# A two-layer GRU and a mixture of experts on one core: another opening, another spread of side work over the steps, and other ends

## The chip, the cores and the metric

The kernel runs on one core of one Trainium2 chip. The metric is device microseconds of one execution; the runs' median is given with its lowest and highest. The profile is of one more execution, with its own time. Engines: PE multiplies matrices, DVE (VectorE) and ACT (ScalarE) work on elements, POOL (GpSimd) issues the indirect DMAs and some small work, SP (SyncE) issues most other DMAs.

## The reference, cut to what matters

Two batches of 1024 tokens, 256 wide. A layer `x = x + L0(x, cond)`, then `x = x + L1(x, cond)`:

```python
# L0
mixed = tanh(x @ W_in.T + b_in + cond)
# a GRU layer: h starts at 0, one step per token
r = sigmoid(xr + hr); z = sigmoid(xz + hz)
n = tanh(xn + r * hn)
h = (1 - z) * n + z * h
# two such layers, one on the other; then
gate = sigmoid(cond @ W_gate.T + b_gate)
out = ((gate + 1) * h2) @ W_out.T + b_out
# L1: 8 experts, 2 of them for each token
shared = (silu(x @ w1) * (x @ w3)) @ w2
s = sigmoid(concat(x, cond) @ router_W)      # top 2 of s + router_bias
routed = sum over the chosen: s_e / sum(s) * (gelu(x @ W1e[e]) @ W2e[e])
out = (shared + routed) / 3
```

## The kernel before

**The recurrence in chunks.** Each sequence is cut into J = 16 chunks of S = 62 tokens, and all 2 x 16 = 32 chunks take a step at once. A chunk's begin is not known, so each layer first takes warm-up steps: `AHEAD = (62, 44)`. Whether all chunk ends fit the begins is counted; if not, a second path (not run here) computes it step by step. The 2048 tokens lie in 64 groups of 32, a group being what one step takes. The first 32 tokens are two extra groups, 0 and 1 (`EXTRA = 2`).

**A tick** is one turn of the loop at L666: a step of layer 0, and from tick 20 on a step of layer 1 that follows it by `LAG = 2`. Ticks 0 to 123 run layer 0, 20 to 125 layer 1. In a step (`finish_scanned`, L320), PE adds the state's product with `whh` (L289) to sums that hold the input's part already; ACT makes the two gates (L330); a DVE scan makes r * hn + xn (L333); ACT's tanh makes n (L344); DVE makes (z - 1) * h (L346); a second scan makes the new row (L349); and DVE transposes it (L362) for the next product. Hooks between these (`before_n`, `after_n`, `between`) take other work, in the order in which the engine's queue gets it. The sign of z's part and of n's weights is turned once, in the weights themselves (`negate`, L193).

**Side work in the ticks.** The step's input comes from `inputs` (four parts per group: bias of the state's part, then r, z, n). Two kinds of pieces make it. A mixing piece (`mix`, L229) makes half of `mixed` for 256 tokens: four products on PE (L238), two tanh on ACT (L250). An input piece (`input_piece`, L418) makes one group: 16 products on PE (L261) and a DVE addition of the biases (L428). `work_of` (L550) gives each tick before layer 1 runs room for three, where a mixing piece counts two, and each later tick one piece, in the order of `pieces_in_turn`; mixing so reaches into the ticks with both layers. `prepare` (L502) has ACT copy a group's inputs into the sums' bank for the next tick (L506); `feed` (L511) adds layer 1's input products (L261 as well).

**Places.** `place(tick, where, what)` hangs other work at a spot of a tick: `product` (on PE, behind layer 0's state product), `n0`, `scan0`, `scan1` (in the hooks of the first or second layer), `end`. Before the change `Front.prepare` (L822: the output gate, the gated output weights, the condition's part of the router) stands at ticks 12 to 16, and the output products of finished groups of 8 (`plan`, L604) follow from tick 71 on. Everything in the loop is issued in the written order (`manual_schedule`, L665).

**Start.** SP's queue loads `w_in`, the first 256 tokens of x, `wih0`, its bias, `whh0`, 256 more tokens, the second bias, `wih1`, `whh1`, the rest of x (1.5 MB in three), then what is used later. Two mixing pieces, DVE's negation in `wih0` and two input pieces stand ahead of tick 0.

**The end of the loop and after.** w1's products for the first part of the shared expert's hidden layer stand at tick 125, its w3 products in `all_of` (L970) for the last group of 8: output products, x added, then the turn to token order, then the router's products. `moe` routes (L1060 to L1195), computes the shared hidden parts, gathers tokens of each expert's block with POOL's indirect DMAs (L1251), multiplies (L1222), writes rows to DRAM (L1268), and gathers them back (L1312), 32 gathers. From the ninth on a one-element POOL copy (L1311) stands ahead of a gather and reads something made just before, which holds the gather behind it. In the last loop (L1340) a product of `w2` per 128 tokens, two gathered rows added (L1326), the sum (L1352), and SP's output DMA (L1353).

Of the kernel before, what the change touches and what calls it, by code (L numbers as in the profile page):

```python
# [17 lines left out]
P = 128  # L18
B = 2
# [22 lines left out]
EXTRA = FIRST // J  # L42

# [40 lines left out]
def gru_moe(ctx, tc, xT, vec, bias, w_in, wih0, whh0, wih1, whh1, w_out, w_gate, router, w1, w3, w2, w1e, w2e, out):  # L84
# [62 lines left out]
    class Steps:  # L147


        def __init__(self, stack, tag, on_pe, rest_of_x):  # L150
# [13 lines left out]
            wih0_sb = weights(wih0, KD, 3 * D, "wih0_sb", gru_only)  # L164
            load_bias(0)
            whh0_sb = weights(whh0, KD, 3 * D, "whh0_sb", gru_only)
# [25 lines left out]

        def negate(self, engine, weights_sb, i):  # L193

            part = weights_sb.rearrange("p k (q g u) -> p (k q) g u", q=Q, g=3)[:, :, i, :]
            engine.tensor_scalar(part, part, -1.0, None, ALU.mult)  # L196
# [32 lines left out]
        def mix(self, n0):  # L229

            mixed = self.mixed_pool.tile([P, KD, MB], FP, name="mixed")
# [22 lines left out]
            return mixed, [piece(m) for m in range(KD)]  # L254
# [65 lines left out]
        def finish_scanned(self, layer, to, tick, before_n, after_n, between, keep=None):  # L320
# [6 lines left out]
            sums = by_sum(ps)  # L327

# [15 lines left out]
            nc.scalar.activation(n[:, :, 0], s[:, 1 : 2 * U : 2], AF.Tanh, scale=-1.0)  # L344
# [13 lines left out]
            if keep is not None:  # L358
                kept = self.edge.tile([P, U], FP, name=f"kept{layer}")
                nc.vector.tensor_scalar(kept, row, keep, None, ALU.mult)  # L360
                row = kept
# [26 lines left out]


    with ExitStack() as stack:  # L390
        g = Steps(stack, "", on_pe=False, rest_of_x=lambda: load_x(MB, TB - MB))
# [6 lines left out]
        for n0 in range(TB, N, TB):  # L398
            load_x(n0, TB)
# [18 lines left out]
        def input_piece(i):  # L418

            ps = g.bank("ps_in")[:, 0 : 3 * U].rearrange("p (c u) -> p c u", c=3)  # L420

            def products():
                at = i * R % MB
                mixed = mixes[i * R // MB]
                return g.times_input(0, ps, lambda k: mixed[:, k, at : at + R], True)

            def rest():
                nc.vector.tensor_tensor(inputs[:, i, 1:4, :], ps, g.sum_bias[0][:, 1:4, :], ALU.add)  # L428
                made.append(i)

            return products, rest, lambda: None
# [28 lines left out]
        nc.vector.tensor_scalar(not_first, not_first, 1.0, None, ALU.min)  # L460
# [72 lines left out]
        mixes, mixed_pieces = {}, []  # L533

        def mix_pieces():
            for i, n0 in enumerate(range(0, N, MB)):
                mixes[i], pieces = g.mix(n0)
                mixed_pieces.extend(pieces)
                yield from pieces

        def input_pieces():
            for i in (*range(EXTRA, MB // R), *range(EXTRA), *range(MB // R, GROUPS)):
                yield input_piece(i)
# [6 lines left out]
        def work_of(tick):  # L550


            if runs(1, tick):
                return take(in_turn, 1)
            room, pieces = 3 - 2 * ((tick, "product") in places), []
            while room > 0:
                new = take(in_turn, 1)
                if not new:
                    break
                pieces += new  # L560
                room -= 2 if new[0] in mixed_pieces else 1
            return pieces
# [6 lines left out]
        def pieces_in_turn():  # L569

            for _ in range(MB // R, GROUPS, MB // R):
                for which in (mixing, making, mixing, *[making] * (MB // R - 1)):
                    yield from take(which, 1)
            yield from making

# [3 lines left out]
        g.negate(nc.vector, g.wih[0], 1)  # L579
        for piece in take(making, 1):  # L580
            for part in piece:
                part()
        g.negate(nc.vector, g.whh[0], 2)
        prepare(0, 0)
        for piece in take(making, 1):
            for part in piece:
                part()
        in_turn = pieces_in_turn()
# [34 lines left out]
        begun = []  # L623

        def begin_hidden():
            pa, last = front.hidden_sums(g.bank, 0, 0, "w1")
            begun.append(pa)
            return last

        place(AHEAD[0] + S + LAG - 1, "product", begin_hidden)  # L630
        for block in range(1, N // MB):
            place(block - 1, "end", lambda block=block: spread(block))
        place(N // MB - 1, "end", lambda: g.sum_of_biases(1, less_z=True))
        for i, (product, end) in enumerate(front.prepare(g.bank)):
            if product:
                place(12 + i, "product", product)
            place(12 + i, "end", end)
# [27 lines left out]
        with tc.manual_schedule():  # L665
            for tick in range(AHEAD[0] + S + LAG):  # L666
# [10 lines left out]
                for layer in now:  # L677
# [3 lines left out]
                    if layer == 0:  # L681
                        last = placed(tick, "product")
                        last = do(work, 0) or last
                        if not busy:
# [6 lines left out]
                            lambda: placed(tick, "n0"),  # L691
                            lambda: copied.append(prepare(0, tick + 1)),
# [5 lines left out]
                    else:  # L698
                        last = feed(tick + 1, range(KD) if busy or 0 not in now else [1])
                        if 0 not in now:  # L700
                            placed(tick, "product")
# [24 lines left out]

            for where in ("n0", "scan0", "end"):
                placed(AHEAD[0] + S + LAG, where)
            sig, silu = (
                g.mixed_pool.tile([P, KD, MB], FP, name="mixed").rearrange("p k n -> p (k n)") for _ in range(2)  # L730
            )
            nc.scalar.activation(sig, begun[0], AF.Sigmoid)
            nc.vector.tensor_tensor(silu, begun[0], sig, ALU.mult)

            def rest_of_hidden():
                pb, _ = front.hidden_sums(g.bank, 0, 0, "w3")
                nc.vector.tensor_tensor(front.hid(0, slice(0, TB)), silu, pb, ALU.mult)

            front.all_of(g.bank, GROUPS // GS - 1, rest_of_hidden)
# [12 lines left out]
    with tc.If(n_fit < P):  # L752
        with ExitStack() as stack:
# [4 lines left out]
            for n0 in range(0, N, MB):  # L758
                mixed, pieces = g.mix(n0)
                for piece in pieces:  # L760
                    for part in piece:
                        part()
# [41 lines left out]
class Front:  # L804
# [17 lines left out]
    def prepare(self, bank):  # L822
# [16 lines left out]
        def gates():  # L839
            for m in range(KD):  # L840
                nc.scalar.activation(
                    self.gate[:, m, :], ps["gate"][:, m, :], AF.Sigmoid, bias=vec_sb[:, B_GATE + m : B_GATE + m + 1]
                )
            nc.vector.tensor_scalar(self.gate, self.gate, 1.0, None, ALU.add)

        def weights(b):
            for k in range(KD):
                nc.vector.tensor_scalar(
                    self.gated_out[:, b, k, :], later["w_out"][:, k, :], self.gate[:, k, b : b + 1], None, ALU.mult
                )  # L850

        def spread():
            for k in range(KD):
                for b in range(B):
                    i = COND + k * B + b
                    nc.vector.tensor_copy(
                        self.cond_b[:, k, :, b, :], vec_sb[:, i : i + 1].unsqueeze(2).to_broadcast([P, P // R, J])
                    )

        def context_sums():  # L860
# [11 lines left out]

        return (
            (gate_sums, gates),
            (None, lambda: weights(0)),
            (None, lambda: weights(1)),
            (None, spread),
            (context_sums, lambda: nc.vector.tensor_copy(self.context, ps["context"])),
# [91 lines left out]
    def all_of(self, bank, group, between=lambda: None):  # L970
# [4 lines left out]
        between()  # L975
# [452 lines left out]
```

## Time and profile before

| | us |
|---|---|
| median of 3 runs | 540.21 (539.62 to 541.03) |
| profiled execution | 539.22 |
| its span, first to last instruction | 537.4 |
| granted TensorE clock, mean | 0.994 |

Busy times of the stages, in us, from the trace's windows:

| stage | from : to | PE | DVE | ACT | POOL |
|---|---|---|---|---|---|
| to the end of tick 0's second scan | 0 : 13.42 | 8.38 | 4.34 | 3.91 | 2.35 |
| layer 0 alone | 13.42 : 67.74 | 53.53 | 37.17 | 21.67 | 4.17 |
| both layers, mixing | 67.74 : 118.22 | 50.01 | 42.21 | 29.55 | 0.43 |
| both layers | 118.22 : 358.09 | 231.24 | 209.93 | 146.25 | 0.61 |
| last two steps, last group | 358.09 : 370.29 | 9.80 | 8.54 | 3.45 | 0.00 |
| routing, shared hidden | 370.29 : 400.02 | 29.33 | 26.31 | 6.09 | 7.66 |
| experts | 400.02 : 478.49 | 77.79 | 27.21 | 27.79 | 28.37 |
| shared hidden, gathers back | 478.49 : 501.19 | 22.55 | 11.32 | 5.61 | 15.09 |
| last products, outputs | 501.19 : 530.63 | 27.79 | 18.34 | 0.10 | 20.73 |
| close | 530.63 : 537.38 | 0.00 | 0.00 | 0.00 | 0.00 |

The profile puts instructions down to a line of the kernel and a tile: `PE ps_step L289` is the product of a step's state. In the order of time, a row's first number is its start, the second how long it (or a run of equal ones, `x16`) lasted, and the brackets tell how long the engine was idle before it and what it waited for. Matmul ends are modelled, so a PE that is busy throughout can still have been waited for or have waited. Idle time of an engine that is off the chain costs nothing.

### The profile page before, as it was taken

Reading aid. Unit: us, or ns where it says so; the run is one execution under the profiler, and the core shown is the slowest. Engines: PE = TensorE matmul, PEld = TensorE weight load, DVE = VectorE, ACT = ScalarE, POOL = GpSimd, SP = SyncE. Lnnn points to the kernel's source line nnn. Section 1 sums busy time; section 2 is a strip of 40 time slices with the busy share of each in tenths; the row PEclk is TensorE's granted clock in tenths of the full one; section 3 lists DMA queues with packets and bytes.
Section 4 is the critical chain, followed back from the end, with each engine's and each line's share of the span. In section 5 each row is a group of like instructions: output and inputs, shape, how many; then the busy total and the mean of one; then the engine's idle time right before and its main releaser. Section 6 shows DMA issues by size and latency. Waiting matters only on the chain.

```text
span 537.4 us, 18538 instructions
## 1 busy us (share of the span) xinstructions
PE 510.4 (95%) x7492; PEld 339.5 (63%) x7492; DVE 385.4 (72%) x1292; ACT 244.4 (45%) x832; POOL 79.4 (15%) x136
## 2 busy tenths in 40 slices
PE   6999999999999999999999999989999999999993
PEld 3666666666654445665666656655448888864783
DVE  3776678989988888888889888887973333324852
ACT  2334356566666556566565665642123333341000
POOL 1200000000000000000000000002054444117881
PEclk9999999999999999999999999999999999999997
DMA  8990000000000000000000000002023433213453
GB/s 276 368 291 3 2 3 2 4 2 4 13 3 2 13 2 4 2 22 3 22 23 2 23 8 17 23 1 80 1 59 118 124 123 119 98 50 105 118 163 94
DMA packets 23087, 32.13 MB, mean 60 GB/s; under 512 B 3040, under 2 KB 18528, under 8 KB 22976
## 3 DMA queue, kind: packets, MB, share of 16 engines
q1 hardware_dynamic: 19632, 22.04, 12.2%
q0 software_dynamic: 3216, 8.79, 5.9%
q8 instruction: 63, 1.03, 0.8%
q14 instruction: 32, 0.26, 0.2%
q10 hardware_dynamic: 144, 0.01, 0.0%
HBM read 21.26 MB, written 9.57 MB: 57 GB/s over the span
## 4 chain that ended last, share of the span: by engine, by line
DVE 43%; PE 32%; ACT 10%; POOL 5%; issue 5%; DMA 3%; SPq 0%; POOLq 0%; DVEq 0%; ACTq 0%
DVE row L349 15%; DVE ps_step L333 14%; DVE h L362 9%; ACT n L344 9%; PE ps_h L1222 6%; PE ps_y L1222 6%; PE ps_step L289 5%; PE ps_in L261 5%; POOL inputs L1312 4%; PE ps_w L947 3%; PE ps_mix L238 3%; DMA x_sb<-in_xT 2%; PE ps_hT L1214 1%; PE ps_xT L1214 1%; DMA inputs<-back,slots 1%
## 5 line engine op out<-in xcount | busy, mean ns | idle before, releaser
L289 PE MATMUL ps_step<-whh_sb,h 128*32 128x192 f32 x3616 | 193.0, 331 | 6.7 <-DVE h L362 6.0
L289 PEld LDWEIGHTS ps_step<-whh_sb,h 128*32 128x32 f32 x3616 | 95.0, 109 | 72.6 <-DVE h L362 52.6
L349 DVE TENSOR_TENSOR_SCAN row<-gates,n 128x128 f32<-128x128 f32 x230 | 97.7, 425 | 31.7 <-ACT n L344 30.9
L261 PE MATMUL ps_step<-wih_sb,h 128*32 128x192 f32 x1696 | 103.2, 328 | 4.7 <-ACT ps_step L506 1.7
L333 DVE TENSOR_TENSOR_SCAN ps_step<-gates,ps_step 128x128 f32<-128x128 f32 x230 | 96.7, 421 | 14.6 <-ACT gates L330 14.4
L344 ACT ACTIVATE n<-ps_step 128x64 f32<-128x64 f32 x230 | 53.6, 233 | 112.9 <-DVE ps_step L333 112.9
L330 ACT ACTIVATE gates<-ps_step 128x128 f32<-128x128 f32 x230 | 66.6, 290 | 34.1 <-PE ps_step L289 27.5
L261 PEld LDWEIGHTS ps_step<-wih_sb,h 128*32 128x32 f32 x1696 | 57.5, 109 | 30.9 <-ACT ps_step L506 18.1
L362 DVE STREAM_TRANSPOSE h<-row 128x64 f32<-128x64 f32 x228 | 56.0, 246 | 8.0
L947 PE MATMUL ps_w<-x_sb,w_sb 128*128 128x512 f32 x128 | 57.0, 596 | 0.1
L261 PE MATMUL ps_in<-wih_sb,mixed 128*32 128x192 f32 x1024 | 51.7, 327 | 2.0 <-DVE wih_sb L196 2.0
L1216 DVE COPY hT<-ps_hT 128x256 f32<-128x256 f32 x35 | 14.9, 425 | 48.8 <-PE ps_hT L1214 48.8
L506 ACT COPY ps_step<-inputs 128x256 f32<-128x256 f32 x124 | 48.1, 388 | 2.9 <-DVE inputs L428 2.9
L346 DVE SCALAR_TENSOR_TENSOR n<-gates,row 128x64 f32<-128x64 f32 x224 | 46.8, 209 | 0.0
L261 PEld LDWEIGHTS ps_in<-wih_sb,mixed 128*32 128x32 f32 x1024 | 33.6, 110 | 12.9 <-issue 4.4
L1251 POOL DMA_INDIRECT inputs<-given,pick x35 | 33.3, 953 | 55.0 <-PE ps_xT L1214 31.6
L506 ACT COPY ps_step<-bt 128x256 f32<-128x256 f32 x106 | 39.9, 377 | 3.3
L947 PEld LDWEIGHTS ps_w<-x_sb,w_sb 128*128 128x128 f32 x128 | 23.7, 190 | 27.1 <-issue 25.6
L1222 PE MATMUL ps_h<-w1e_sb,xT 128*128 x140 | 36.1, 380 | 0.7 <-DVE xT L1216 0.7
L1222 PE MATMUL ps_y<-w2e_sb,hT 128*128 x140 | 35.9, 379 | 0.0
L1312 POOL DMA_INDIRECT inputs<-back,slots x32 | 31.5, 984 | 29.2 <-DMA back<-y 20.5
L1222 PEld LDWEIGHTS ps_y<-w2e_sb,hT 128*128 128x128 f32 x140 | 26.5, 190 | 4.6 <-DVE hT L1216 1.0
(175 smaller groups left out, 425.2 us busy)
## 6 DMA issues: line engine op xcount, KB each, us to landing
back<-y SPq DMA_DIRECT2D x35, 128.0 KB, 1.7
w1e_sb<-in_w1e SPq DMA_DIRECT2D x1, 2048.0 KB, 14.9
w2e_sb<-in_w2e SPq DMA_DIRECT2D x1, 2048.0 KB, 18.8
given<-inputs SPq DMA_DIRECT2D x8, 256.0 KB, 2.1
out_dram<-inputs SPq DMA_DIRECT2D x16, 128.0 KB, 2.1
wih_sb<-in_wih SPq DMA_DIRECT2D x2, 768.0 KB, 8.7
whh_sb<-in_whh SPq DMA_DIRECT2D x2, 768.0 KB, 10.1
x_sb<-in_xT SPq DMA_DIRECT2D x3, 512.0 KB, 11.2
```

Of the source, the lines that this page charges most:

```text
L261: last = nc.tensor.matmul(out=out[cols(q), :, :], lhsT=given(k), rhs=self.wih[layer][:, k, q * 3 * U : (q + 1) * 3 * U].rearrange("p (g u) ...
L289: nc.tensor.matmul(out=by_sum(self.sums[layer])[cols(q), 0:3, :], lhsT=self.states[layer][:, k, :], rhs=self.whh[layer][:, k, q * 3 * U : ...
L330: nc.scalar.activation(gates[:, :, :, 1], sums[:, 1:3, :], AF.Sigmoid)
L333: nc.vector.tensor_tensor_scan(s, gates[:, 0, :, :].rearrange("p u i -> p (u i)"), ps[:, 0 : 6 * U : 3], 0.0, ALU.mult, ALU.add,)
L344: nc.scalar.activation(n[:, :, 0], s[:, 1 : 2 * U : 2], AF.Tanh, scale=-1.0)
L346: nc.vector.scalar_tensor_tensor(n[:, :, 1], gates[:, 1, :, 1], 1.0, h, ALU.subtract, ALU.mult)
L349: nc.vector.tensor_tensor_scan(row.rearrange("p u i -> p (u i)"), gates[:, 1, :, :].rearrange("p u i -> p (u i)"), n.rearrange("p u i -> p ...
L362: nc.vector.transpose(to, row)
L506: return nc.scalar.copy(by_sum(banks[layer][tick % 2])[:, 0:4, :], g.sum_bias[1] if layer else inputs[:, group_of(0, tick), :, :],)
L947: last = self.tc.nc.tensor.matmul(out=ps, lhsT=self.later[name][:, k, m * P : (m + 1) * P], rhs=self.x1[:, k, blk * TB : (blk + 1) * TB], ...
L1222: nc.tensor.matmul(out=ps, lhsT=of[:, k, :], rhs=weights_sb[:, bass.ds(e * KD + k, 1), :], start=(k == 0), stop=(k == KD - 1),)
L1312: nc.gpsimd.indirect_dma_start(out=yb, out_offset=None, in_=back[:, :], in_offset=bass.IndirectOffsetOnAxis(ap=slots[:, i % 2, i // 2 : i ...
```

## The change

- `wih0` is loaded in two halves with the bias between them; the three loads of the rest of x move ahead of the second bias, `wih1` and `whh1`.
- Ahead of tick 0 nothing is negated any more. The first two input pieces are multiplied with the plain weights; `less_z` subtracts where the negated weight would have been used, and the first group's sums go from PSUM into tick 0's bank at once. Tick 0's end makes the group's stored inputs and negates `wih0` on DVE; ACT negates `whh0` behind tick 0's tanh.
- `mixed` is written into `hs1`, layer 1's state tensor, instead of a pool of two tiles. `work_of` gives ticks 1 to 14 one mixing and one input piece, 15 to 18 three input pieces, 19 two, later ticks one until they are all made.
- The reset of the first chunk's rows is made ahead of a step, on the state and as the tanh's scale, instead of behind it.
- `Front.prepare` moves from ticks 12 to 16 to ticks 54 to 62, cut into smaller parts, in the hooks rather than at the tick's end.
- w1's first hidden products move to tick 123 and the first half of w3's to tick 124, in a new place `behind` (behind layer 1's products); the silu follows at tick 124's end. In `all_of` the router's products come ahead of the turns.
- The one-element copy stands only ahead of every second gather (11 instead of 23). The outputs are issued from ACT's queue instead of SP's.

```diff
-            wih0_sb = weights(wih0, KD, 3 * D, "wih0_sb", gru_only)
+            wih0_sb = gru_only.tile([P, KD, 3 * D], FP, name="wih0_sb")
+            wih0_v = wih0.rearrange("(k p) m -> p k m", p=P)
+            nc.sync.dma_start(out=wih0_sb[:, 0, :], in_=wih0_v[:, 0, :])
             load_bias(0)
+            nc.sync.dma_start(out=wih0_sb[:, 1, :], in_=wih0_v[:, 1, :])
...
+            if keep is not None:
+                kept = self.edge.tile([P, U], FP, name=f"kept{layer}")
+                nc.vector.tensor_scalar(kept, h, keep, -1.0, ALU.mult, ALU.mult)
+                h = kept
...
-            nc.scalar.activation(n[:, :, 0], s[:, 1 : 2 * U : 2], AF.Tanh, scale=-1.0)
+            nc.scalar.activation(n[:, :, 0], s[:, 1 : 2 * U : 2], AF.Tanh, scale=-1.0 if keep is None else keep)
...
-            if keep is not None:
-                kept = self.edge.tile([P, U], FP, name=f"kept{layer}")
-                nc.vector.tensor_scalar(kept, row, keep, None, ALU.mult)
-                row = kept
...
+        def less_z(ps, to):
+
+            biases = g.sum_bias[0][:, 1:4, :]
+            nc.vector.tensor_tensor(to[:, 0:3:2, :], ps[:, 0:3:2, :], biases[:, 0:3:2, :], ALU.add)
+            nc.vector.scalar_tensor_tensor(to[:, 1, :], ps[:, 1, :], -1.0, biases[:, 1, :], ALU.mult, ALU.add)
...
-                return g.times_input(0, ps, lambda k: mixed[:, k, at : at + R], True)
+                return g.times_input(0, ps, lambda k: hs1[:, k, cols(i)], True)
...
+                if EXTRA <= i < EXTRA + PLAIN:
+                    less_z(ps, inputs[:, i, 1:4, :])
...
-                mixes[i], pieces = g.mix(n0)
...
+                yield from g.mix(n0, hs1[:, :, n0 : n0 + MB])
...
-                return take(in_turn, 1)
-            room, pieces = 3 - 2 * ((tick, "product") in places), []
...
+                return take(making, 1)
+            mixed = take(mixing, 1) if tick else []
+            return mixed + take(making, 1 if mixed or not tick else 2 if runs(1, tick + 1) else 3)
...
-        g.negate(nc.vector, g.wih[0], 1)
...
-        g.negate(nc.vector, g.whh[0], 2)
...
+        first_sums = by_sum(banks[0][0])
+        nc.scalar.copy(first_sums[:, 0, :], g.sum_bias[0][:, 0, :])
+        first_ps = by_part(g.bank("ps_in"))
+        (products, _, _), (next_products, next_rest, _) = input_piece(EXTRA, first_ps), input_piece(EXTRA + 1)
+        products()
+        next_products()
+        less_z(first_ps, first_sums[:, 1:4, :])
+        next_rest()
...
+        place(last_tick - 2, "behind", lambda: begin_hidden("w1", range(KD)))
+        place(last_tick - 1, "behind", lambda: begin_hidden("w3", [0]))
+        place(last_tick - 1, "end", silu)
...
+        place(0, "end", lambda: less_z(first_ps, inputs[:, EXTRA, 1:4, :]))
+        place(0, "end", lambda: g.negate(nc.vector, g.wih[0], 1))
...
+                place(AHEAD[0] - 8 + i, where, what)
+        def negate_first():
+
+            part = g.of_gate(g.whh[0], 2)
+            nc.scalar.mul(part, part, -1.0)
...
+                            lambda: placed(tick, "n0") if tick else copied.append(prepare(0, 1)),
+                            lambda: copied.append(prepare(0, tick + 1)) if tick else negate_first(),
...
+            {"product": gate_sums, "scan1": lambda: spread(0)},
+            {"n0": gates, "scan1": lambda: spread(1)},
+            {"scan0": add_one},
+            *({"scan0": lambda b=b, k=k: weights(b, k)} for b in range(B) for k in range(KD)),
+            {"product": context_sums},
+            {"scan0": keep_context},
...
         between()
+        self.route(bank, group)
+        self.keep_logits(group)
+        behind()
...
-        self.route(bank, group)
-        self.keep_logits(group)
...
-        if behind is not None:
+        if behind is not None and i % 2 == 0:
             nc.gpsimd.tensor_copy(yb[0:1, 0:1], behind[0:1, 0:1])
...
-            nc.sync.dma_start(out=out[j * P : (j + 1) * P, :], in_=base[:, j, :])
+            nc.scalar.dma_start(out=out[j * P : (j + 1) * P, :], in_=base[:, j, :])
```

## The prediction

> **What bounds the kernel now.** I read the page first, then busy times by stage, then the order of time, stage by stage.
>
> ```profile
> PE 510.4 (95%) x7492; PEld 339.5 (63%) x7492; DVE 385.4 (72%) x1292; ACT 244.4 (45%) x832; POOL 79.4 (15%) x136
> ...
> DVE row L349 15%; DVE ps_step L333 14%; DVE h L362 9%; ACT n L344 9%; PE ps_h L1222 6%; PE ps_y L1222 6%; PE ps_step L289 5%; PE ps_in L261 5%; POOL inputs L1312 4%; PE ps_w L947 3%; PE ps_mix L238 3%; DMA x_sb<-in_xT 2%; PE ps_hT L1214 1%; PE ps_xT L1214 1%; DMA inputs<-back,slots 1%
> ```
>
> PE is busy 95%, yet the chain that ends last runs through DVE's scans and transposition and ACT's tanh: a step waits for the step before it. The transposition L362 closes a step, so the distance between two layer-0 rows of L362 is one tick. In the order of time I took all of them: 2.79 to 2.81 us while layer 0 runs alone (ticks 1 to 19), 2.74 with both layers (most of ticks 21 to 61), 2.72 to 2.79 later. The longer ones are what there is to win: tick 1 (3.35), 5 (3.12), 13 and 14 (2.95, 2.96), 20 (3.25), 24, 26, 34, 36 (3.44 to 3.47), 29 (3.03), 32 (2.94), 62 and 64. One of them, in the order of time:
>
> ```profile
> 79.24 0.24 DVE L362 STREAM_TRANSPOSE h<-row 128x64 f32<-128x64 f32 x1
> ...
> 82.71 0.24 DVE L362 STREAM_TRANSPOSE h<-row 128x64 f32<-128x64 f32 x1
> ...
> 83.79 1.13 PE L238 MATMUL ps_mix<-x_sb,w_in_sb 128*128 128x256 f32 x4
> ...
> 84.85 0.86 PE L289 MATMUL ps_step<-whh_sb,h 128*32 128x192 f32 x16
> ...
> 85.44 0.24 DVE L362 STREAM_TRANSPOSE h<-row 128x64 f32<-128x64 f32 x1
> ```
>
> The layer-0 rows are 79.24, 82.71 and 85.44: tick 24 took 3.47, tick 25 2.73. A mixing product at 83.79 holds PE while a layer-1 state, transposed from 84.03 to 84.27, waits for its product until 84.85; so tick 26 will be long too. Start and end, same view:
>
> ```profile
> 9.23 0.43 DVE L196 TENSOR_SCALAR wih_sb<-wih_sb 128x512 f32<-128x512 f32 x1 [5.87 <-DMA wih_sb<-in_wih]
> ...
> 11.84 0.29 ACT L330 ACTIVATE gates<-ps_step 128x128 f32<-128x128 f32 x1
> ...
> 12.54 1.10 PE L238 MATMUL ps_mix<-x_sb,w_in_sb 128*128 128x256 f32 x4 [1.28 <-DMA x_sb<-in_xT]
> ...
> 13.42 0.25 DVE L362 STREAM_TRANSPOSE h<-row 128x64 f32<-128x64 f32 x1
> ...
> 14.25 0.83 PE L289 MATMUL ps_step<-whh_sb,h 128*32 128x192 f32 x16
> ...
> 525.70 0.98 POOL L1312 DMA_INDIRECT inputs<-back,slots x1 [0.27 <-POOL inputs L1311]
> ...
> 527.96 1.03 PE L1344 MATMUL ps_s<-w_sb,inputs 128*128 128x256 f32 x4
> ...
> 529.48 0.48 DVE L1326 SCALAR_TENSOR_TENSOR inputs<-inputs,share 128x256 f32<-128x256 f32 x1 [1.38 <-DMA inputs<-back,slots]
> 529.88 0.75 DVE L1352 SCALAR_TENSOR_TENSOR inputs<-ps_s,inputs 128x256 f32<-128x256 f32 x2
> ```
>
> The first step waits for weights, then for their negation; the end waits for POOL's last gather, not for PE, done at 528.99. POOL then waits for that gather (landed 529.35), and its closing drain runs 531.04 to 536.59, the last thing before the span ends.
>
> **The parts and their costs** (plus is time won).
>
> 1. *Start, +1.3.* Whole weights landed at 9.21, bias at 9.74. The second half now stands behind the bias with the same bytes ahead, so 9.75. PE has done the first half by then; eight products for the second take 0.35 and 0.2 to land (half of a 16-instruction piece, 0.66 apart): 10.35. The negation (0.43) is off this path, two sums in its place: 0.28 (L187's row) and 0.21, overlapping, 0.4. Gates at 10.85, not 11.84. Behind them DVE holds the next piece's two sums (0.4), so the scan starts about 11.45; ACT's copy for tick 1 (0.38) now stands ahead of the tanh, still inside the scan. Transposition about 12.65, against 13.42: 0.77. whh0 (landed 11.71) is negated on ACT behind the tanh, 128x512, about 0.6 by its 0.38 for 256 columns: 12.7, inside the transposition. Tick 0 then has no mixing product that waits for x until 12.42; that held tick 1's step from about 13.72 to 14.25: another 0.53. DVE's added work behind tick 0 (two pairs of sums, 0.4 each, and wih0's negation) ends about 14.05, before tick 1's scan at 14.25. Bounds 0.5 (halves bring nothing) and 1.8 (they land at 9.21). SP has one issue more (0.47), but landings run to 20.97 against issues to 10.1, so bytes set them. The three x loads (1.5 MB) pass bias1, wih1 and whh1: at 768 KB in 1.98 us (14.90 to 16.88) these land 4 us later, POOL's negations follow near 21, needed at tick 20 (67 us). That gap hides them.
> 2. *Preparation out of ticks 12 to 16, +0.3* (2.95 + 2.96 less 2 x 2.79), bounds 0 and 0.33.
> 3. *Two pieces instead of three in tick 19, +0.5.* PE was 0.65 over there; tick 20 goes from 3.25 to 2.77. Bounds 0 and 0.5.
> 4. *Mixing in ticks 1 to 14, +2.9.* Four ticks fall to 2.74: 3.47 + 3.47 + 3.44 + 3.47 - 4 x 2.74. What comes in their place, one input piece per tick up to 52, is free: ticks 38 to 44 carried one at 2.74. A single-layer tick with mixing and one piece has 0.82 + 1.06 + 0.92 = 2.8 of PE, and lasted 2.79 (ticks 4, 9, 10). Bounds 2.3 and 2.9.
> 5. *The kept rows, +0.1.* They cost 0.29 and 0.20 behind the scan (ticks 29, 32). Ahead of the first scan DVE has no gap either (L362 to L333 0.17 to 0.23), so 0.1 to 0.2 comes back, and tanh with a scale per partition gets 0.08 longer (mixed, with a bias per partition, 366 ns; gates of the same size 290). Bounds -0.1 and 0.5.
> 6. *Preparation in ticks 54 to 62, -0.5.* Its DVE parts fit between L346 and L349, as the input sums (0.34) do; two gate activations (0.42) fit in ACT's 0.49 wait. PE's eight gate products (0.98) stand between a four-product row of 0.71 that costs about 0.04 a tick and mixing's 1.13 that costs 0.73; nearest to mixing. Bounds 0 and -0.73.
> 7. *Last ticks, +0.6.* w1's products (1.82) start near 358.1 in a 1.54 us PE gap, so tick 124's step moves from 359.75 to about 359.95; w3's first half (0.9) and the turn hold tick 125 by about 0.3. The last products start near 365.6 instead of 365.82, half of w3 (0.9) behind them is gone: 0.6 by the start of the 64 shared products (370.29), where PE is busy 29.33 of 29.73 to 400.02. Silu's 0.60 and 0.69 fill a gap of DVE before 363.79. The routing chain starts 1 us earlier, but its gathers waited for PE already. Bounds -0.2 and 1.9 (all w1 and half w3 hidden, no delay).
> 8. *Gathers and output queue, +2.2.* Of 23 one-element copies 12 go. A gather behind one starts 1.44 after the last, without one 1.25: 12 x 0.19 = 2.3. The last gather starts near 523.4 and lands near 526.9; the last sum is then held by PE's 528.99, so the output leaves at 529.6 instead of 530.75. If the drain goes with the gather, 2.3; if with the output, 1.15. ACT has finished its last activation at 501.3, nothing is queued behind the outputs. I take 2.2; bounds 1.0 and 2.4.
>
> Sum: 1.3 + 0.3 + 0.5 + 2.9 + 0.1 - 0.5 + 0.6 + 2.2 = 7.4. The profiled execution took 539.22 (span 537.4 and 1.8 around it), so 531.8; the runs' median, 540.21, is 0.99 above it, so 532.8. Bounds alone: 10.4 down to 2.8 won, 529.8 to 537.4.
>
> **The rivals.**
>
> A. *The halves pay a fixed time.* The 9 KB vec_sb, issued at 0.80 with nothing ahead, landed at 2.98: 2.2 us are fixed. If the second half pays that behind the first, it lands near 11.95, the gates come 1.2 later than before, and part 1 turns from 1.3 to -0.9: 535.0. Against it: bias landed 0.53 behind wih0 on the same queue.
>
> [...]
>
> B. *The end hangs on PE and the outputs*, the drain with them: part 8 gives 1.0, so 534.0. For it: PE has no pause from 478.49 to 528.99. Against: SP was through its closing waits at 535.40, the drain at 536.59.
>
> C. *Every tick from 1 to 14 pays for its mixing.* Tick 5 had a scan 0.33 late beside a mixing tanh; 14 x 0.33 = 4.6, so 537.4. Against: the other such ticks had no delay.
>
> D. *Slower: layer 1's transposition waits for PE.* Its target hs1 now also holds the mixed inputs that PE reads. If L362 waited for PE's newest product in that tensor, not for the one that read its columns, it would wait for the feed behind it: in the tick at 149.69 that ended 150.17, half a microsecond. Over the 62 first writes (ticks 20 to 81) that is 31 us: 563.8; from 0.12 a tick on the kernel is slower. Against: from tick 71 on, products read hs1 while L362 writes it, at 2.73 to 2.79.
>
> **How the numbers follow.** Forecast 0.62 (532.8; by itself 530.2 to 534.5), A 0.09, B 0.11, C 0.08, D 0.07, gains that cancel 0.03. Within 0.3% (1.6 us) is about what a measurement of this kernel can tell from no change. Faster 0.90, same 0.03, slower 0.07. The range, 530.2 to 536.8, takes in A and B and most of the bounds, and leaves out C, D and the corners.
>
> **What would show it.** Gates of tick 0 near 10.9 and L362 of tick 1 near 15.5 (part 1); ticks 24, 26, 34, 36 at 2.74 (4); tick 55 about 0.5 long (6); the first of the 64 shared products about 11.7 after tick 123's L362, against 12.2 (358.09 to 370.29; 7); 11 copies L1311, the last gather about 41.4 after the first, against 43.67, and the drain earlier by as much (8). The forecast is wrong if wih0's second half lands past 10.5, if single-layer ticks pass 2.9 with a mixing product, if the two-layer tick is not 2.74, or if the drain does not move.

## The result, and the profile after

The changed kernel took 538.00 us (median of 11, 537.09 to 539.23) where the kernel before took 540.21 (median of 11): a ratio of 0.9952, interval 0.9941 to 0.9964. It is faster by 2.2 us, not by the 7.4 forecast, and lies outside the range of 530.2 to 536.8. In the profiled execution the span is 536.8 us against 537.4.

The page after, its engines and its chain. The chain now breaks off at 476.06; what it holds from there to the end is nearly all PE:

```profile
PE 512.1 (95%) x7492; PEld 341.2 (64%) x7492; DVE 385.1 (72%) x1296; ACT 243.6 (45%) x833; POOL 76.9 (14%) x124
...
PE ps_s L1367 6%; PE ps_w L969 4%; DVE inputs L1375 0%
```

Every line of the code moved down; L369 is the old L362, L341 the gates (L330), L355 the tanh (L344), L360 the closing scan (L349), L526 the copy into PSUM (L506), L981 to L983 the shared expert's activation (L959 to L961), L1335 the gather (L1312), L1334 its one-element copy (L1311), L1349 the addition of the gathered rows (L1326), L1367 the last products (L1344), L1375 the last sums (L1352). In the order of time, the start and ticks 24 to 26:

```profile
10.56 0.28 ACT L341 ACTIVATE gates<-ps_step 128x128 f32<-128x128 f32 x1 [1.53 <-DVE ps_step L434]
...
12.06 0.24 DVE L369 STREAM_TRANSPOSE h<-row 128x64 f32<-128x64 f32 x1
...
14.91 0.24 DVE L369 STREAM_TRANSPOSE h<-row 128x64 f32<-128x64 f32 x1
...
79.61 0.24 DVE L369 STREAM_TRANSPOSE h<-row 128x64 f32<-128x64 f32 x1
...
82.35 0.24 DVE L369 STREAM_TRANSPOSE h<-row 128x64 f32<-128x64 f32 x1
...
85.10 0.24 DVE L369 STREAM_TRANSPOSE h<-row 128x64 f32<-128x64 f32 x1
```

Tick 0 closes at 12.06 instead of 13.42, tick 1 at 14.91 instead of 16.76; ticks 25 and 26 take 2.74 and 2.75 (26 took 3.47). Tick 123 closes at 353.80 instead of 358.09 and the first product of the last stage starts at 496.79 instead of 501.19: 4.4 us were won by then, and the forecast had 5.2. The last stage then lost most of it. Busy times of that stage, before and after (the columns are the engines' busy us, the granted clock of PE, the share of the DMA engines and GB/s):

```profile
501.19:528.98 27.79, 27.79 (x129) 24.13 (x127) 17.19 (x40) 0.10 (x1) 20.73 (x34) 1.00 0.54 158
```

```profile
496.79:503.00 6.21, 6.21 (x30) 5.34 (x29) 0.69 (x1) 0.60 (x1) 4.35 (x8) 1.00 0.30 84
503.00:506.66 3.66, 1.75 (x6) 0.91 (x5) 2.45 (x5) 0.00 (x0) 2.91 (x3) 1.00 0.39 110
506.66:513.50 6.84, 5.60 (x14) 4.49 (x15) 4.71 (x12) 0.00 (x0) 2.48 (x4) 0.50 0.29 92
513.50:531.12 17.62, 17.62 (x82) 15.18 (x80) 9.87 (x24) 0.00 (x0) 8.52 (x12) 1.00 0.53 161
```

The same 16 tiles take 34.33 us instead of 27.79. PE stands still three times (0.46, 1.05 and 1.65 us: 3.16) and has a granted clock of 0.50 for 6.84 us, in which it is busy for 5.60. Over the stage it is busy for 31.17 us instead of 27.79: 3.38 more, and with the pauses the 6.54 lost. The trace shows the order in time: the clock falls at 506.66, 0.40 into the longest pause, after 3.66 us in which PE was busy for 1.75, and is back at 1.00 from 513.50 on. In series 3 below the changed kernel paused for 1.7 us in all, 0.4 at the longest, and kept its clock (0.997 in the mean of the execution, 0.991 here); without copies, in the same series, PE was busy for 33.00 of 49.52 us of this stage, at a mean clock of 0.79. What sets the clock was not shown. What stands beside the pauses, in the order of time, DVE and POOL:

```profile
494.96 1.00 DVE L1349 SCALAR_TENSOR_TENSOR inputs<-inputs,share 128x256 f32<-128x256 f32 x2
500.86 0.69 DVE L982 TENSOR_TENSOR silu<-ps_w,sig 128x512 f32<-128x512 f32 x1 [4.90 <-ACT sig L981]
503.70 0.69 DVE L983 TENSOR_TENSOR inputs<-silu,ps_w 128x512 f32<-128x512 f32 x1 [2.15 <-remote]
...
508.65 0.42 DVE L1375 SCALAR_TENSOR_TENSOR inputs<-ps_s,inputs 128x256 f32<-128x256 f32 x1 [2.43 <-remote]
...
509.90 0.42 DVE L1375 SCALAR_TENSOR_TENSOR inputs<-ps_s,inputs 128x256 f32<-128x256 f32 x1
...
511.15 0.42 DVE L1375 SCALAR_TENSOR_TENSOR inputs<-ps_s,inputs 128x256 f32<-128x256 f32 x1
```

```profile
505.37 1.15 POOL L1335 DMA_INDIRECT inputs<-back,slots  x1 [0.30 <-issue]
510.38 0.36 POOL L1334 COPY inputs<-inputs 1x1 f32<-1x1 f32 x1 [3.87 <-DVE inputs L1375]
511.08 1.00 POOL L1335 DMA_INDIRECT inputs<-back,slots  x1 [0.33 <-POOL inputs L1334]
```

The kernel before shows no wait (no brackets) ahead of its first sum:

```profile
505.45 0.42 DVE L1352 SCALAR_TENSOR_TENSOR inputs<-ps_s,inputs 128x256 f32<-128x256 f32 x1
```

After the change the first sum waits until 508.65. It waits for PE's own semaphore alone (the row says "remote" because no instruction of PE ends near the update), yet PE's rows let the eight products of its tile end at 498.67. The next sums follow 1.25 us apart without a wait, though the eight products of a tile take 1.73 at full clock: those products must have been there, and only the news of them came late, for four tiles at once. Three things go with it: ACT is idle 6.71 us ahead of the last hidden part's sigmoid and DVE behind it; PE pauses where its rows name no wait ("issue"), each time among the eight products of one tile; and POOL's copy ahead of the 23rd gather waits 3.87 us for the second tile's sum, so 5.7 us pass between two gathers.

The page shows another sign of it. The landing times of most transfers are missing. A line of the page before, and two of the page after:

```profile
back<-y SPq DMA_DIRECT2D x35, 128.0 KB, 1.7
```

```profile
back<-y SPq DMA_DIRECT2D x35, 128.0 KB
w1e_sb<-in_w1e SPq DMA_DIRECT2D x1, 2048.0 KB
```

The trace holds 4,663 semaphore updates where that of the kernel before holds 5,478; those of PE that are there arrive at 500.16, 503.68 and then four within 0.3 us from 508.62 on.

### The profile page after: what moved, and what is told of

Its sections match the earlier page's. It is cut to its first block, busy times and chain, and to the rows that moved or that the text cites. A ratio compares the mean times of both kernels' runs of the same rounds, so it can differ in the third digit from the quotient of the medians.

```text
span 536.8 us, 18511 instructions
## 1 busy us (share of the span) xinstructions
PE 512.1 (95%) x7492; PEld 341.2 (64%) x7492; DVE 385.1 (72%) x1296; ACT 243.6 (45%) x833; POOL 76.9 (14%) x124
## 5 line engine op out<-in xcount | busy, mean ns | idle before, releaser
L360 DVE TENSOR_TENSOR_SCAN row<-gates,n 128x128 f32<-128x128 f32 x230 | 98.0, 426 | 29.6 <-ACT n L355 28.3
L344 DVE TENSOR_TENSOR_SCAN ps_step<-gates,ps_step 128x128 f32<-128x128 f32 x230 | 97.3, 423 | 15.0 <-ACT gates L341 15.0
L268 PE MATMUL ps_step<-wih_sb,h 128*32 128x192 f32 x1696 | 99.7, 328 | 4.1 <-ACT ps_step L526 2.4
L355 ACT ACTIVATE n<-ps_step 128x64 f32<-128x64 f32 x228 | 53.0, 232 | 111.0 <-DVE ps_step L344 110.9
L341 ACT ACTIVATE gates<-ps_step 128x128 f32<-128x128 f32 x230 | 66.5, 289 | 35.5 <-PE ps_step L296 26.0
L369 DVE STREAM_TRANSPOSE h<-row 128x64 f32<-128x64 f32 x230 | 56.5, 246 | 8.0
L268 PE MATMUL ps_in<-wih_sb,h 128*32 128x192 f32 x1024 | 54.4, 328 | 1.8 <-ACT h L257 1.4
L526 ACT COPY ps_step<-inputs 128x256 f32<-128x256 f32 x123 | 47.8, 389 | 0.0
L268 PEld LDWEIGHTS ps_in<-wih_sb,h 128*32 128x32 f32 x1024 | 34.0, 110 | 14.6 <-issue 4.6
L526 ACT COPY ps_step<-bt 128x256 f32<-128x256 f32 x106 | 39.9, 376 | 3.3
L1335 POOL DMA_INDIRECT inputs<-back,slots x32 | 30.9, 964 | 30.0 <-issue 28.3
```

Source lines behind the costliest of these rows:

```text
L268: last = nc.tensor.matmul(out=out[cols(q), :, :], lhsT=given(k), rhs=self.wih[layer][:, k, q * 3 * U : (q + 1) * 3 * U].rearrange("p (g u) ...
L341: nc.scalar.activation(gates[:, :, :, 1], sums[:, 1:3, :], AF.Sigmoid)
L344: nc.vector.tensor_tensor_scan(s, gates[:, 0, :, :].rearrange("p u i -> p (u i)"), ps[:, 0 : 6 * U : 3], 0.0, ALU.mult, ALU.add,)
L360: nc.vector.tensor_tensor_scan(row.rearrange("p u i -> p (u i)"), gates[:, 1, :, :].rearrange("p u i -> p (u i)"), n.rearrange("p u i -> p ...
L369: nc.vector.transpose(to, row)
L526: return nc.scalar.copy(by_sum(banks[layer][tick % 2])[:, 0:4, :], g.sum_bias[1] if layer else inputs[:, group_of(0, tick), :, :],)
```

## The experiments

The kernels of one series ran one after the other on one chip, with their own runs of the kernel before. All ratios are to the kernel before of the same series. "Late" says that the traces lack some 800 updates and that the first sum comes 6.3 us or more behind the first product of the last stage; "timely", that no updates are missing and it comes at most 5.0 us behind. The kernel before was traced twice, for the table ahead of the change and in series 2, and was timely both times. Whether it is late too in a late series no trace shows; its medians there, 540.21 to 541.75, are longer than the 539.22 and 539.40 of the timely ones.

| series | before, us | changed kernel | other kernels | updates |
|---|---|---|---|---|
| result | 540.21 | 0.9952 | | late |
| 1 | 540.80 | | outputs on SP 0.9943, all copies 0.9932, both undone 0.9914, part 8 alone 1.0032 | late |
| 2 | 539.22 | | no copies 0.9863, copies in the hidden loop only 0.9872 | timely |
| 3 | 541.45 | 0.9909 | part 8 alone 1.0000, both undone 0.9916, no copies 1.0215 | late |
| 4 | 541.75 | 0.9922 | part 8 alone 1.0009, both undone 0.9913, hidden loop only 1.0138 | late |
| 5 | 539.40 | 0.9864 | | timely |

**Series 1: which edit of the last stage?** The loss lies behind 496.8, so I undid its two edits singly and together, and put them alone into the kernel before.

```
-            nc.scalar.dma_start(out=out[j * P : (j + 1) * P, :], in_=base[:, j, :])
+            nc.sync.dma_start(out=out[j * P : (j + 1) * P, :], in_=base[:, j, :])
```

> The changed kernel with its output transfers issued by SP again, all else as changed. In the changed kernel 4.4 us of the gain are there when the first product of the last stage starts (496.79 against 501.19), and that stage then takes 34.3 us instead of 27.8. Theory Q, ACT's issuing of the outputs costs the time: this kernel's last stage is back near 28 us and the whole near 540.2 - 4.4 - (0 to 2.3 for the 12 copies) = 533.5 to 535.8. Theory P, the denser gathers (12 copies fewer) cost it: the stage stays near 34 us and the kernel near 538. Theory S, neither, something that the earlier start of this stage brings: near 538 too.

Measured 537.63 (0.9943, interval 0.9923 to 0.9963), last stage 496.11 to 529.85. Theory Q falls: the queue of the outputs is not the cause.

```
-        if behind is not None and i % 2 == 0:
+        if behind is not None:
```

> The changed kernel with a one-element copy ahead of every gather again (23 copies instead of 11), outputs still on ACT's queue. Theory P, the denser gathers cost the time: the last stage is back near 28 us, PE has no pause in it, and the kernel takes about 540.2 - 4.4 = 535.8, less up to 1 us. Theory Q (ACT's queue): the stage stays near 34 us, the kernel near 538. Theory S (the earlier start): near 538.

Measured 536.78 (0.9932, 0.9916 to 0.9949); the last stage takes 27.92 us and PE's rows show no pause. But the first sum still waits for PE until 502.38, and the one after it 0.82: the copies do not make PE's updates timely. This trace is of the fastest execution (534.70), and the interval overlaps that of the variant before it, so the times alone do not show that the copies matter.

Both of these edits together:

> The changed kernel with both edits of the last stage undone: a copy ahead of every gather, and outputs on SP. What stays is parts 1 to 7. Theories P and Q, one of the two edits costs the time: about 540.2 - 4.4 = 535.8 and a last stage of 28 us. Theory S, neither does: 538 or more, with PE pausing in the last stage as in the changed kernel.

Measured 535.82 (0.9914, 0.9894 to 0.9934): parts 1 to 7 alone give 5.0 us, against 5.2 forecast. The first sum waits for PE until 503.70, so the lateness is not made by the two edits.

The kernel before with the two edits of the last stage alone:

> The kernel before with only the two edits of the last stage: a copy ahead of every second gather, and outputs on ACT's queue. By the prediction's part 8 it is 2.2 us faster than before, 538.0. Theories P and Q: the last stage is 34 instead of 28 us long, and the kernel about 0.6 - (-3.8) slower, near 544. Theory S, the loss comes only with the earlier start: 538 to 540.

Measured 542.52 (1.0032, 1.0017 to 1.0046), with PE's four pauses and 5.98 us between the 22nd and 23rd gather. So part 8 costs 1.7 us where it was to bring 2.2, without any of the other parts.

**Series 2: is it in the kernel before, and is it the density of the gathers?** First the kernel before once more, then the changed kernel with outputs on SP and three densities of copies. Without any copy:

> The kernel before, unchanged, profiled once more. In the changed kernel and in the four variants of it the updates of PE's own semaphore reach DVE late in the last stage: the first sum of the last stage waits for PE until 502.4 to 508.7, though the profile lets the four products end near 498. In the kernel before no instruction of DVE waits for PE there (first sum at 505.45, idle 0). If the lateness comes only with the change (earlier start, fewer copies), this run shows the old picture: first sum near 505.4 with no idle time ahead of it. If it belongs to this stage of either kernel, the first sum waits 1 to 2 us for PE here too.

Span 537.1; first sum at 505.08 without a wait, 5,478 updates: the old picture.

```
-                fetch_back(made)
+                fetch_back()
...
-            fetch_back(base[:, j - 1, :] if j else None)
+            fetch_back()
```

> The changed kernel with outputs on SP and without any one-element copy ahead of a gather. Density theory, the closer the gathers follow each other the later PE's updates come, and that alone sets the end: later than with half of the copies, 538 or more. Waiting theory, the loss is that POOL's copy in the sum loop waits for the sum before it, which is late (the gap of 5.7 to 6.1 us between the 22nd and the 23rd gather): without copies there is nothing to wait for, the last gather is issued about 39 us after the first (31 x 1.26), near 516, PE sets the end, and the kernel takes 533 to 535.5.

Measured 531.62 (0.9863, 0.9846 to 0.9879), last gather 39.91 us after the first, first sum at 498.60 without a wait. I read this as the waiting theory proved; it was not, as series 3 shows.

Only the second of the two replacements, and a copy ahead of every gather in the loop over the hidden parts:

> The changed kernel with outputs on SP, a copy ahead of every gather in the loop over the shared hidden parts, and none in the loop over the sums. Waiting theory: the first 20 gathers come as in the kernel before, the last 12 at 1.26 us without a wait for a sum; the last one about 41 us after the first, near 518, and the kernel near 533 to 535. Density theory: the dense gathers now lie beside the products of the last stage and make these late: 536.5 or more.

Measured 532.29 (0.9872, 0.9855 to 0.9888); the first sum does not wait for PE either.

Two copies ahead of every gather:

```
             nc.gpsimd.tensor_copy(yb[0:1, 0:1], behind[0:1, 0:1])
+            nc.gpsimd.tensor_copy(yb[0:1, 1:2], behind[0:1, 1:2])
```

> The changed kernel with outputs on SP and two one-element copies ahead of every gather instead of one. Density theory: the gathers come 1.63 us apart, DVE's first sum no longer waits for PE (idle under 0.5, against 1.8 with one copy), and the last gather, not PE, sets the end: about 23 x 0.19 = 4.4 later, 539 to 540. If the lateness has nothing to do with the gathers, the first sum still waits 1.8 us or more for PE, with the same end.

538.35 in one execution: last gather 47.39 us after the first, first sum at 501.38 without a wait. Gathers 1.55 us apart make the last gather the end. But none of the four kernels of this series had late updates, whatever its density, so nothing is said yet on where these come from.

**Series 3: the same kernels again, side by side.** No edit is new.

> The changed kernel, unchanged, beside three variants on one chip. Theory W, the copies themselves cost the time (the copy in the sum loop that waits for a late sum, with the gap of 5.7 to 6.1 us between the 22nd and the 23rd gather): the gap is there again, PE's updates come late again, the ratio to the kernel before is 0.995. Theory D, the late updates of PE (first sum waiting until 508.65) are a disturbance of the executions measured so far, which four other executions did not have, and the copies only made it dearer: without it the first sum comes near 500 with no wait for PE, the last gather near 477 + 41.4 = 518.5, and the kernel takes 7 us less than before, a ratio near 0.987.

536.30 (0.9909, 0.9885 to 0.9932), first sum at 505.29, pauses of 3.44 and 3.33 us between gathers: late.

> The kernel before with only the two edits of the last stage, once more. Theory W: slower than before again, ratio 1.003, with a gap of 6 us between the 22nd and the 23rd gather. Theory D: no such gap, no late update of PE, and the 2.2 us that part 8 of the prediction gives: ratio 0.996.

541.41 (1.0000, 0.9985 to 1.0015): late, and part 8 brings nothing.

> The changed kernel with both edits of the last stage undone, once more. Both theories: 4.4 to 5.0 us less than before, ratio 0.991. Theory W: faster than the changed kernel beside it by 2 us. Theory D: slower than the changed kernel beside it by 2 us, and first sum without a wait for PE (before: waited 1.76).

537.01 (0.9916, 0.9899 to 0.9932): late; no different from the changed kernel beside it.

> The changed kernel without any copy and with outputs on SP, once more, on the chip that runs the other three. Theory W: 5 to 6 us faster than the changed kernel. Theory D: in undisturbed executions PE's last product (523.8) already sets its end, so it is within 1 us of the changed kernel; in disturbed ones it is the one with the late updates that no copy waits for, and stays below 536.

553.27 (1.0215, 1.0198 to 1.0232): the fastest kernel of series 2 is the slowest here, 21.7 us apart. Its last stage in the order of time, DVE and POOL:

```profile
516.42 1.92 DVE L1349 SCALAR_TENSOR_TENSOR inputs<-inputs,share 128x256 f32<-128x256 f32 x4
522.17 0.42 DVE L1375 SCALAR_TENSOR_TENSOR inputs<-ps_s,inputs 128x256 f32<-128x256 f32 x1 [3.84 <-remote]
...
523.43 0.42 DVE L1375 SCALAR_TENSOR_TENSOR inputs<-ps_s,inputs 128x256 f32<-128x256 f32 x1
```

```profile
515.95 0.95 POOL L1335 DMA_INDIRECT inputs<-back,slots  x1 [0.30 <-issue]
```

The first product started at 496.13 and the first sum at 522.17: only after the last gather does the news come through, and then six sums run 1.25 us apart. Neither theory as I wrote it holds. Theory W is refuted by the timely series, where no copy costs anything; theory D's claim that the kernel without copies stays below 536 is refuted by 553. What fits both, and was not tested by itself: in some series PE's updates are held up while gathers are issued, the longer the denser they are.

**Series 4: the changed kernel once more, and the hidden loop's copies under late updates.**

> The changed kernel a third time. If PE's updates are in time (no missing updates in the trace): first sum near 500 without a wait for PE, last gather 41.4 us after the first, 7 us faster than before (ratio 0.987). If they are late: gap of 3 to 6 us in the gathers, ratio 0.991 to 0.995.

537.28 (0.9922, 0.9894 to 0.9951): late, first sum at 508.56, 5.76 us between two gathers.

> The kernel before with only the two edits of the last stage. Updates in time: part 8 as forecast, 2.2 us faster than before (ratio 0.996). Late: ratio 1.000 to 1.003 as in the two earlier runs.

541.60 (1.0009, 0.9986 to 1.0033): late.

> The changed kernel with both edits of the last stage undone. Either way 4.4 to 5 us faster than before, ratio 0.991; with updates in time it is 2 us slower than the changed kernel, with late ones 0 to 2 us faster.

536.74 (0.9913, 0.9888 to 0.9938): late, first sum at 505.93.

> The changed kernel with outputs on SP, copies ahead of every gather in the loop over the hidden parts and none in the loop over the sums. Updates in time: 532.3 again (ratio 0.987). Late ones: if the density in the hidden loop sets the lateness, first sum at 503 to 504 as with all copies, no copy waits for it, and the kernel stays near 535; if the dense gathers beside the sums make PE late as without any copy, 540 or more.

549.38 (1.0138, 1.0112 to 1.0164): the gathers 1.25 us apart beside the sums hold them up, the third sum waiting 10.65 us, until 523.36, 4.3 after the last gather. The late traces together, by the time from the first product of the last stage to the first sum: with all copies 6.3 to 9.5 us (gathers 1.43 to 1.52 apart), with half 9.0 to 12.1 (1.28 and 1.40), with none 26.0 (1.25). In the timely ones it is 2.6 to 5.0 at any density.

**Series 5: the changed kernel where updates are timely.**

> The changed kernel a fourth time. PE's updates in time: first sum near 500 without a wait for PE, last gather 41.4 us after the first, ratio 0.987. Late: a pause of 3 to 6 us between two gathers, ratio 0.991 to 0.995.

531.85 (0.9864, 0.9847 to 0.9880): 7.55 us faster than the kernel before. 5,490 updates, no pause of PE, gathers over 41.23 us. Busy times of its last stage, and its end in the order of time:

```profile
495.92:523.71 27.79, 27.79 (x129) 24.13 (x127) 17.24 (x41) 0.00 (x0) 18.07 (x25) 1.00 0.52 158
```

```profile
498.61 0.42 DVE L1375 SCALAR_TENSOR_TENSOR inputs<-ps_s,inputs 128x256 f32<-128x256 f32 x1
...
518.03 0.95 POOL L1335 DMA_INDIRECT inputs<-back,slots  x1 [0.31 <-issue]
...
522.69 1.03 PE L1367 MATMUL ps_s<-w_sb,inputs 128*128 128x256 f32 x4
523.75 0.42 DVE L1375 SCALAR_TENSOR_TENSOR inputs<-ps_s,inputs 128x256 f32<-128x256 f32 x1 [1.30 <-PE ps_s L1367]
```

> The changed kernel with outputs on SP and two copies ahead of every gather, once more. Where PE's updates are in time: as before, first sum near 501.4 without a wait, 538.4. Where they are late in the kernel beside it: if the density of the gathers delays them, 1.55 us between gathers instead of 1.43 leaves the first sum before 503.5 with a wait under 1.5 (with one copy 503.7 to 505.9), and the last gather sets the end, 538 to 539; if the density has no part in it, the first sum waits as with one copy, and the kernel takes 540 or more.

537.40 in one execution, timely: it repeats series 2, and says nothing on whether 1.55 us between gathers is slow enough where updates are late. That stays open.

No version beats the changed kernel in both kinds of series: without copies it is level in the timely ones (0.9863 against 0.9864) and loses 17 us in the late one; with both edits undone it is level in series 3 and 4, where both kernels ran (the 2 us by which series 1 is better than the result lie between two series), and was not measured in a timely one.

## Why the prediction was wrong, point by point

The step that failed is **part 8**. It priced the copies and the queue from a profile in which DVE never waited for PE's products, took it that a gather without a copy only comes earlier (its bounds of 1.0 and 2.4 leave no room for a loss), and never asked what the remaining copies wait for. In the result's trace PE's updates were late, and a copy in the loop over the sums waits for a sum; over the late traces the delay is longer where the gathers are denser. Part 8 brought -3.8 in the profiled execution instead of +2.2, and by the ratios -1.7, 0.0 and -0.5 where it was put alone into the kernel before (the last two not told apart from none). Why PE's updates come late in some series stays open. In the timely series the sum of the forecast came out, 531.85 against 532.8 (7.55 won, 7.4 forecast).

The parts can be priced there, from the kernel before profiled again (span 537.09) to the changed kernel (529.23), by the times at which both reach the same point:

| up to | before | changed | won so far | step, us | forecast |
|---|---|---|---|---|---|
| tick 1 closes | 16.45 | 14.58 | 1.87 | part 1: +1.87 | +1.3 |
| tick 16 | 59.08 | 56.79 | 2.29 | part 2: +0.42 | +0.3 |
| tick 20 | 70.71 | 67.98 | 2.73 | part 3: +0.44 | +0.5 |
| tick 36 | 117.92 | 112.24 | 5.68 | parts 4, 5: +2.95 | +3.0 |
| tick 54 | 167.21 | 161.83 | 5.38 | tick 45: -0.30 | none |
| tick 64 | 195.51 | 190.45 | 5.06 | part 6: -0.32 | -0.5 |
| tick 123 | 357.65 | 353.15 | 4.50 | ticks 81, 105: -0.56 | none |
| first expert's turn | 399.65 | 394.75 | 4.90 | part 7: +0.40 | +0.6 |
| first last product | 500.82 | 495.92 | 4.90 | 0.0 | |
| end of span | 537.09 | 529.23 | 7.86 | part 8: +2.96 | +2.2 |

1. *Start*: undersized, just above its bound of 1.8, and near only because two errors offset each other. The forecast has the products wait for the second half of `wih0` until 9.75. In the timely trace that half landed at 8.12 (in the kernel before of this pair the whole weights landed at 8.88), and PE waited for something else: the tanh that makes `mixed` stands in ACT's queue behind the new copy of the bias into tick 0's sums, and that copy waits for the bias:

```profile
7.41 0.22 ACT L586 COPY ps_step<-bt 128x64 f32<-128x64 f32 x1 [4.64 <-DVE bt L191]
...
7.56 1.14 ACT L257 ACTIVATE h<-ps_mix,mix_bias 128x128 f32<-128x128 f32 x4
...
8.23 2.34 PE L268 MATMUL ps_in<-wih_sb,h 128*32 128x192 f32 x46 [1.07 <-ACT h L257]
```

So the products of the first half, done by then in the forecast, had not begun when the second half landed. The gates came at 10.22 (11.51 in the kernel before of this pair; 10.56 and 11.84 in the pair of the result), 0.3 earlier than worked out, and DVE began the scan 0.32 behind the gates, not 0.6. The 0.53 of tick 1 came nearly as said: 2.85 instead of 3.36. Rival A is dead: the halves were not paid for.
2. and 3. Right: ticks 13 and 14 at 2.79, tick 20 at 2.80.
4. and 5. Right: ticks 24, 26, 34 and 36 fell to 2.73 to 2.75 (2.86 won), ticks 29 and 32 by 0.09 and 0.02. Single-layer ticks with a mixing product take 2.79, so rival C is dead. Only tick 5 is long, 3.13, as before the change (in the result's trace tick 3 as well, 3.08). Rival D is dead as well: two-layer ticks stay at 2.74.
6. Right in kind: tick 55 takes 3.13 instead of 2.73, 0.40.
7. The first of the 64 shared products comes 11.46 us behind tick 123's transposition (before: 12.20; forecast 11.7); 0.40 of this reaches the experts.
8. Here, timely: 2.41 by the gathers (41.23 instead of 43.64; forecast 2.3), and 0.60 because the last one lands 3.11 us after its issue and not 3.71. The drain moved with it, 530.70 to 522.83. Rival B, with the end on PE and the outputs, did not come in this execution, by little: SP was through its closing waits at 528.16 and the drain at 528.38. Without any copy, in series 2, it did: the drain ended at 526.94 and the span at 529.70, so that the denser gathers brought nothing more. In the result's execution it came in a worse form: the drain ended at 533.62, and outputs behind PE's last product set 536.8.

Missed altogether: ticks 45, 81 and 105 are 0.25 to 0.29 longer. In tick 45 of the timely trace the closing scan is released by the copy behind the tanh, which ends at 136.67, and not by the tanh, which ends at 136.39:

```profile
136.16 0.23 ACT L355 ACTIVATE n<-ps_step 128x64 f32<-128x64 f32 x1 [0.49 <-DVE ps_step L344]
136.28 0.39 ACT L526 COPY ps_step<-inputs 128x256 f32<-128x256 f32 x1
...
136.71 0.42 DVE L360 TENSOR_TENSOR_SCAN row<-gates,n 128x128 f32<-128x128 f32 x1 [0.21 <-ACT ps_step L526]
```

The kernel before shows the same in tick 5. Why in these ticks was not looked into.

## What to carry to other kernels

A small instruction that only spaces transfers out can be holding something else in time: before it is removed, ask what the neighbouring engines' waits look like with the transfers closer, and what the remaining ones wait for, since a transfer that waits for a sum which waits for a late engine closes a ring (here a copy waited 3.87 us for a sum, behind one that had waited 2.43 us for PE). Price a last stage from more than one execution, and book the gain stage by stage, by the times at which both kernels reach the same point: that showed within one profile that the parts ahead of the last stage had come out. Look whether the trace is complete, since missing updates were the first sign of the lateness here.

## What the runs showed of the hardware that was not expected

Under gathers issued from POOL every 1.25 to 1.5 us, PE's semaphore updates reach ACT and DVE up to 24 us after the modelled end of the products (498.02 to 522.15 in series 3 without copies) in four of six series, then come all at once (four within 0.3 us); in the other two they come on time at every density tried. The same kernel took 531.6 and 553.3 us in two series. Series 4 and 5 ran under the same chip number, so that number does not tell them apart. The transfers themselves are not slower: the packets of a gather end 2.3 to 3.7 us after its issue in the late executions and 2.3 to 4.0 in the timely ones.

What makes a series late is open. Wherever PE was late, the trace also lacked updates (4,607 to 4,723 instead of 5,476 to 5,500), and only from the first gather on (the experts' first, at 388.55 in the result's trace): up to it every trace of the changed kernel and of its variants, late or timely, holds 2,834. Whether the recording has a part in the lateness was not shown: no run here separates the recording from the work, since every execution that was timed was recorded.
